# Where layer 1's second chunk keeps its results, and two places in the order of work: a two-layer convolution kernel

## The chip, the cores and the metric

The kernel runs on one core of one Trainium2 chip. The metric is the device time of one execution in microseconds (us); a profiled execution gives, besides its time, the span from its first to its last instruction and the mean clock that was granted to TensorE.

## The reference, cut to what matters

The input x has shape (4, 64, 256, 256). Layer 0 normalises it by groups of channels, runs a gated mixture of small experts behind a 3x3 convolution, and adds the result to x. Layer 1 normalises again and runs two 3x3 convolutions, each followed by a batch normalisation over all four images:

```python
    # --- layer 0 (conv_preact) ---
    x = x + _L0_conv_ref(_gn(x), ...)
    # --- layer 1 (conv_preact) ---
    x = x + _L1_conv_ref(_gn(x), ...)
    ...
    h = _conv3x3(x, _quantize_weight(w1), b1)
    h = jax.nn.relu(_batchnorm(h, gamma1, beta1))
    h = _conv3x3(h, _quantize_weight(w2), b2)
    h = _batchnorm(h, gamma2, beta2)
    return jax.nn.relu(h + identity)
```

In layer 0, a convolution gives h, a 1x1 convolution splits it in two, one half goes through a horizontal and a vertical filter of three taps and a GELU (this is xs), the other half through the experts' low ranks; the experts' sum and xs are projected and added to x. Because a batch normalisation needs the statistics of all images, all of layer 1's first convolution has to be done before its second can begin.

## The kernel before, in words

**Stages.** The four images ("batches" b) are each cut into 16 chunks k of 16 rows; two rows of 64 channels fill the 128 partitions. The time falls into four stages: layer 0's front (to about 1290 us), layer 1's first convolution, called conv1 (to about 1987 us), its second, conv2 (to about 2550 us), and a last stage that reads y and h2 back, normalises and writes the output. The second half of layer 0 (the projection and the sum y = x + ..., called out here) lags behind: its last ten slots of batch 2 (n = 22 to 31) and all 32 slots of batch 3 run in the middle of conv1.

**The order of the work** is written by hand. A plan maps a pair (step, order) to calls (`at`, L120), and when it is complete the calls are made in the order of these keys. Each engine keeps that order in its own queue: PE, DVE (VectorE), ACT (ScalarE), POOL (GpSimd), and SP, which issues most DMAs. So a step number says what comes before what on one engine, not a time; semaphores do the rest. Step `CONV1` = 128, called t below for batch 0, is where conv1 begins; a chunk of conv1 takes four steps. The front's last work is spread over the first steps of conv1 by a table, `TAIL`: for the last chunk but one, the taps' t on ACT (`front_taps_i`, L692) is at (t, 13.3), the rest of the taps on DVE (`front_taps_h`, L699 to L717) at (t, 13.4), and xs on ACT (`front_xs`, L723) at (t, 13.5).

**One chunk of conv1.** `conv1_load` (L905, SP) fetches yn, rows of y, from memory. `conv1_differences` (L343, POOL) makes differences d of rows. `conv1_upper_odd` (L923, L359, ACT) and `conv1_upper` (L346, ACT) round the rows and the differences to the format that PE multiplies fast; `conv1_lower_odd` (L362, DVE) and `conv1_lower` (L353, DVE) keep what the rounding lost. PE then makes `conv1_odd` (ps_hm, 12 matmuls) and twice `conv1_even` (ps_h, 12 matmuls each, g = 0 and 1), all on L296. `conv1_shared` (L312, ACT) turns ps_hm into m; `conv1_out` (L318, DVE) makes h from ps_h and m for g = 0 and 1; `conv1_square` (L382, ACT) adds up squares and then has ACT's queue store h to memory (L985, h_d<-h in the profile).

**Places in SBUF.** A tile with a tag and `bufs=1` has one place; a new tile with the tag waits until all readers and stores of the last one are done. h of a chunk goes into tag "h1" of the conv1 pool (one place), or, for odd k outside the first chunks, into tag "x" of the first pool (one place; in the front it held loads of the out work, `xs_load` with place "x", L837). m goes into tag "k" from chunk (0,2) on, which is also the place of layer 0's rank product, stored by `low_store` (L770, SP, low_d<-k).

**The out work.** `out_load` (L828, SP) reads x's rows into a y tile (tag "o", two places); `xs_load` (L837) and `low_load` (L847) fetch xs and the ranks; a slot n projects on PE (ps_o, L506), adds to y on DVE (L873) and takes statistics (L878). After every second slot `out_store` (L886, SP) writes y to memory (y_d<-y). The function `plan_out_late` places this work in conv1: a slot at its step, with order 13.6, the loads nine and six steps ahead, the store one step behind. An issue on SP whose wait isn't over holds every later issue on SP.

**What the change touches:** `conv1_out` (L961 to L963), the line of `plan_out_late` that places `out_store` (L1195 and L1196), and three lines of `plan_conv1` (L1232, L1233, L1235).

Of the kernel before, what the change touches and what calls it, by code (L numbers as in the profile page):

```python
# [41 lines left out]
def conv_preact_kernel(ctx: ExitStack, tc: tile.TileContext, io, col128, colset, col64):  # L42
# [25 lines left out]
    def flat(t):  # L68
        return t.rearrange("p a b -> p (a b)")
# [23 lines left out]
    def chunk_x(name):  # L93
        return first_pool.tile([P, CPAIR, PW], F32, tag="x", name=name, bufs=1)
# [25 lines left out]
    def at(step, order, call, *args):  # L120
        plan[step, order].append((call, args))
# [194 lines left out]
    def leave(h, ps, m, w, total):  # L316

        nc.vector.scalar_tensor_tensor(  # L318
            h.rearrange("p (e k) w -> p e (k w)", e=2),
            ps.rearrange("p e k w -> p e (k w)"),  # L320
            w_scale[w],
            m.unsqueeze(1).to_broadcast([P, 2, GF]),
            ALU.mult,
            ALU.add,
            **({} if total is None else {"accum_out": total}),
        )
# [45 lines left out]
    def totals_less(name, rows):  # L372

        first = stat.tile([P, 6], F32, tag="first", name=f"first_{name}")
        nc.vector.bn_stats(first, rows)
        mv = stat.tile([P, 2], F32, tag="first_mv", name=f"first_mv_{name}")
        nc.vector.bn_aggr(mv, first)
        nc.vector.tensor_scalar(less[name], mv[:, 0:1], -1.0, None, ALU.mult)
# [514 lines left out]
    def out_end(b):  # L893
        gn2[b] = const.tile([P, 3], F32, name=f"gn2_{b}")
        yield from group_norm(st_y.pop(b), c128("avg4"), gn2[b][:, 0:2], f"y{b}", nc.gpsimd if b < B - 2 else nc.vector)
        (nc.gpsimd if b < B - 2 else nc.vector).tensor_scalar(gn2[b][:, 2:3], gn2[b][:, 0:1], gn2[b][:, 1:2], -1.0, ALU.mult, ALU.mult)
# [63 lines left out]

    def conv1_out(b, k, g):  # L961
        if g == 0:
            if k % 2 and (b > 0 or k > 2):  # L963
                h_out[b, k] = flat(chunk_x(f"h1_{b}_{k}"))[:, 0 : CPAIR * W].rearrange("p (a b) -> p a b", b=W)
            else:
                h_out[b, k] = conv1_pool[0].tile([P, CPAIR, W], F32, tag="h1", name=f"h1_{b}_{k}", bufs=1)
        h = h_out[b, k]
        at_h = h[:, 4 * g : 4 * g + 4, :]
        first = k == g == 0
        total = sums[b][:, 2 * k + g : 2 * k + g + 1]  # L970
        leave(at_h, open_h.pop((b, k, g)), m_in[b, k][:, g], "w1", None if first else total)
        if first:
            nc.vector.tensor_reduce(total, h[:, 1:4, :], AX.XY, ALU.add)
            nc.vector.tensor_reduce(sums[b][0:C, NOCT : NOCT + 1], h[0:C, 0, :], AX.X, ALU.add)
            if b == 0:
                totals_less("h1", h[:, 1:3, :])
        if g:
            del m_in[b, k]
# [59 lines left out]
    def at_each(places, chain):  # L1038

        for place in places:  # L1040
            at(*place, next, chain, None)
# [145 lines left out]
    def plan_out_late(b, ns, steps, order, end):  # L1187

        for n, step in zip(ns, steps):
            if n % 2 == 0:  # L1190
                at(step - 9, 0.2, low_load, b, n // 2)
                at(step - 9, 0.3, xs_load, b, n // 2, "h")
                at(step - 6, 0.4, out_load, b, n // 2)
            at(step, order, out_slot, b, n)
            if n % 2:  # L1195
                at(step + 1, 13.3, out_store, b, n // 2)  # L1196
        at_each(end, out_end(b))

    def conv1_first():
# [12 lines left out]
    def plan_conv1(b):  # L1212
        t = CONV1 + b * (NG + 1)
        if b == 0:
            at(t - 4, -1, conv1_first)
            at(t, 12, conv1_open)
        for k in range(NCH):
            T = t + 4 * k
            places = [T + p for p in (-13, -7, -6, -5, -4, -4, -4, -3)]
            if b == 0 and k < 3:  # L1220
                places = [t + p for p in ((-6, -3, -3, -2, -2, -2, -1, -1), (-4, -1, -1, 0, 0, 0, 0, 1), (-2, 1, 2, 3, 4, 4, 4, 5))[k]]
            load, diff, odd, up0, up1, low_odd, low0, low1 = places

            first = b == k == 0

            def late(step, order):
                return (step, 5.5 + (order - 13) if step < t else order)

            at(load, 0, conv1_load, b, k)
            at(*late(diff, 13.08), conv1_differences, b, k)  # L1230
            at(*late(odd, 13.36 if b == 0 and k == 3 else 13.1), conv1_upper_odd, b, k)
            at(*late(up0, 13.12), conv1_upper, b, k, 0)  # L1232
            at(*late(up1, 13.14), conv1_upper, b, k, 1)  # L1233
            at(*late(low_odd, 13.2), conv1_lower_odd, b, k)
            at(*((t, 1.3) if first else late(low0, 13.22)), conv1_lower, b, k, 0)  # L1235
            at(*((t, 1.32) if first else late(low1, 13.24)), conv1_lower, b, k, 1)
            at(T, 1.9 if first else 13, conv1_odd, b, k)
            at(T + 4 / 3, 13, conv1_even, b, k, 0)
            at(T + 4 / 3, 13.15, conv1_shared, b, k)
            at(T + 8 / 3, 13, conv1_even, b, k, 1)  # L1240
            at(T + 8 / 3, 13.05, conv1_out, b, k, 0)
            at(T + 4, 13.05 if k < NCH - 1 else 12.9, conv1_out, b, k, 1)
            at(T + 4 + 4 / 3, 13.16, conv1_square, b, k)
        at(t + NG, 12.95, conv1_end, b)
        at(t + NG + 1, 13.06, conv1_end_out, b)
        at(t + NG + 3, 13.3, conv1_close, b)

    plan_front()
    for b in range(B):
        if b < B - 1:  # L1250
            plan_stats(b + 1)
            plan_out(b, NOCT if b < B - 2 else 22)
            if b == B - 2:
                plan_out_late(b, range(22, NOCT), [CONV1 + 16 + 4 * n for n in range(10)], 13.6, [(CONV1 + n, 12.6) for n in (56, 58, 58, 60, 60, 60, 62)])
        else:
            t, e = CONV1 + 56, CONV1 + b * (NG + 1) - 10
            steps = [t + (e - 6 - t) * n // (NOCT - 1) for n in range(NOCT)]
            plan_out_late(b, range(NOCT), steps, 13.6, [(e - i, 15) for i in (5, 3, 3, 1, 1, 1, -1)])
        plan_conv1(b)
# [116 lines left out]
    with tc.manual_schedule(  # L1376
# [8 lines left out]
        n = len(chunks)  # L1385
# [186 lines left out]
```

## Time and profile before

| | |
|---|---|
| median of 3 runs | 2990.66 us (2983.44 to 2991.94) |
| the profiled execution | 2990.48 us |
| its span | 2988.7 us, mean granted TensorE clock 0.915 |
| PE, matmuls | 2351.9 us busy (79% of the span) |
| DVE | 2440.1 us (82%) |
| ACT | 2024.8 us (68%) |
| POOL | 1682.5 us (56%) |
| DMA | 915.33 MB, mean 306 GB/s |

Busy shares are means over stages with different limits, so they are read stage by stage. In an instruction's row of a timeline the first two numbers are its start from the beginning of the span and its length in us; then follow engine, line, operation, the tiles it writes and reads, and, in brackets, how long the engine was idle before it and what ended that. A row of the chain of waits has start, length and what the time went to; "DMA a<-b" is a transfer that somebody waited for, from its issue to the end of the wait. A row of the waits names the waiter, what it waited for, the total in us, how many times, and the longest.

### The profile page before, as it was taken

To read this page: it belongs to the slowest core of one execution; us is meant where nothing else is said; L and a number is where in the kernel's file an instruction comes from. 1 tells how busy PE (TensorE), PEld (TensorE's weight loads), DVE (VectorE), ACT (ScalarE), POOL (GpSimd) and SP (SyncE) were. 2 spreads that over 40 slices of the span, in tenths; PEclk is the share of its full clock that TensorE was granted. 3 is DMA by queue.
4 is the path that set the end of the run, shared out by engine and by line. 5 is a ranking of instruction groups with operands and counts; after the bars stand their busy time and mean duration, and the time that the engine had idled before them with its cause. 6 is when DMAs were issued, how large, how long until landed. Compare 5 with 4: busy or idle time off the path is not lost.

```text
span 2988.7 us, 52829 instructions
## 1 busy us (share of the span) xinstructions
PE 2351.9 (79%) x21576; PEld 1500.3 (50%) x21576; DVE 2440.1 (82%) x2754; ACT 2024.8 (68%) x2210; POOL 1682.5 (56%) x1283
## 2 busy tenths in 40 slices
PE   1888899999999999989999999989999999100000
PEld 1444445444444555546666667867888888000000
DVE  5678678878878888868988889979999898876665
ACT  6777888778776665567666667968888888432222
POOL 5888888778778888734544546735555565000000
PEclk9999999999999999999999999989999999555555
DMA  8565579999999899849999997747777763899999
GB/s 348 206 237 209 196 270 370 357 350 353 345 336 321 295 320 323 293 181 323 361 345 358 340 337 275 283 164 269 262 266 263 264 234 140 354 420 425 425 424 407
DMA packets 135570, 915.33 MB, mean 306 GB/s; under 512 B 14944, under 2 KB 15712, under 8 KB 40608
## 3 DMA queue, kind: packets, MB, share of 16 engines
q1 hardware_dynamic: 107680, 777.74, 70.1%
q10 hardware_dynamic: 27648, 134.23, 11.3%
q8 instruction: 169, 2.77, 0.4%
q14 instruction: 73, 0.60, 0.1%
HBM read 573.74 MB, written 338.17 MB: 305 GB/s over the span
## 4 chain that ended last, share of the span: by engine, by line
PE 50%; DMA 27%; DVE 10%; POOL 6%; ACT 3%; issue 3%; SPq 0%; ACTq 0%; DVEq 0%; POOLq 0%
PE ps_h L296 19%; PE ps_c L506 8%; PE ps_a L506 6%; PE ps_h2m L296 6%; DMA y<-in_xp 6%; DMA y_d<-y 5%; PE ps_o L506 5%; DMA y_end<-y_d 5%; DMA out<-h 4%; DMA h<-h_d 4%; PE ps_hm L296 3%; POOL x L554 2%; DMA xs_in<-xs_d 2%; DVE y L873 1%; DVE t L707 1%
## 5 line engine op out<-in xcount | busy, mean ns | idle before, releaser
L296 PE MATMUL ps_h<-diff,w_q 128*128 128x512 f32 x3072 | 756.8, 401 | 17.6 <-DVE h L318 17.2
L296 PEld LDWEIGHTS ps_h<-diff,w_q 128*128 128x128 f32 x3072 | 578.9, 190 | 196.1 <-issue 28.8
L506 PE MATMUL ps_c<-v,us 64*64 64x256 f32 x9216 | 538.4, 382 | 28.6 <-DVE ps_c L637 23.8
L343 POOL TENSOR_TENSOR d<-yn 128x1024 f32<-128x1024 f32 x128 | 347.8, 2738 | 305.6 <-DMA yn<-y_d 189.8
L506 PEld LDWEIGHTS ps_c<-v,us 64*64 64x64 f32 x9216 | 359.3, 135 | 180.5 <-DVE ps_c L637 24.2
L506 PE MATMUL ps_a<-h,av 64*64 64x512 f32 x4080 | 388.0, 494 | 55.2 <-DVE t L710 40.1
L343 POOL TENSOR_TENSOR d<-h 128x1024 f32<-128x1024 f32 x127 | 311.9, 2478 | 194.8 <-DVE diff L351 133.3
L318 DVE SCALAR_TENSOR_TENSOR h<-ps_h,scale_w,m 128x1024 f32<-128x1024 f32 x256 | 322.8, 1279 | 73.3 <-PE ps_h L296 53.4
L554 POOL TENSOR_TENSOR x<-x 128x512 f32<-128x512 f32 x256 | 330.0, 1289 | 12.5
L1453 ACT ACTIVATE v<-y_end,shift,gn 128x2048 f32<-128x2048 f32 x64 | 133.8, 2093 | 280.2 <-DMA y_end<-y_d 245.1
L506 PEld LDWEIGHTS ps_a<-h,av 64*64 64x64 f32 x4080 | 153.8, 133 | 331.6 <-issue 203.5
L382 ACT ACTIVATE junk<-h,less_h 128x2048 bf16<-128x2048 f32 (+3 forms) x133 | 255.9, 1924 | 11.1 <-DVE h L318 10.9
L1454 DVE SCALAR_TENSOR_TENSOR h<-h,ss,v 128x2048 f32<-128x2048 f32 x64 | 149.8, 2349 | 121.4 <-ACT v L1453 96.8
L692 ACT ACTIVATE t<-ps_a,tap_bias,m 128x1016 f32<-128x1016 f32 x128 | 153.4, 1199 | 128.7 <-PE ps_a L506 99.7
L873 DVE SCALAR_TENSOR_TENSOR y<-ps_o,ob,y 128x1024 f32<-128x1024 f32 x128 | 163.9, 1280 | 74.8 <-PE ps_o L506 26.8
L723 ACT ACTIVATE xs<-t 128x1024 f32<-128x1024 f32 x128 | 134.8, 1053 | 102.3 <-DVE t L710 88.4
L296 PE MATMUL ps_h2m<-odd,w_q 128*128 128x512 f32 x768 | 193.2, 401 | 8.2 <-DVE odd L362 4.4
L296 PE MATMUL ps_hm<-odd,w_q 128*128 128x512 f32 x768 | 191.4, 398 | 2.8 <-DVE t L710 1.3
L353 DVE SCALAR_TENSOR_TENSOR diff<-d,gn,diff 128x1024 fp32r<-128x1024 f32 x128 | 192.3, 1531 | 0.5 <-ACT diff L346 0.5
L346 ACT ACTIVATE diff<-d 128x1024 fp32r<-128x1024 f32 x128 | 135.1, 1056 | 83.3 <-POOL d L343 82.1
L546 POOL TENSOR_TENSOR x<-x,x 128x512 f32<-128x512 f32 x128 | 160.9, 1280 | 22.2 <-ACT x L540 22.2
L296 PEld LDWEIGHTS ps_h2m<-odd,w_q 128*128 128x128 f32 x768 | 146.3, 191 | 44.5 <-DVE odd L362 5.2
(250 smaller groups left out, 4271.5 us busy)
## 6 DMA issues: line engine op xcount, KB each, us to landing
x<-in_xc SPq DMA_DIRECT2D x64, 1280.0 KB
h<-h_d SPq DMA_DIRECT2D x64, 1152.0 KB
yn<-y_d SPq DMA_DIRECT2D x60, 1152.0 KB
xs_in<-in_xp SPq DMA_DIRECT2D x64, 1024.0 KB
xs_d<-xs ACTq DMA_DIRECT2D x128, 512.0 KB
xs_in<-xs_d SPq DMA_DIRECT2D x64, 1024.0 KB
y<-in_xp SPq DMA_DIRECT2D x64, 1024.0 KB
y_d<-y SPq DMA_DIRECT2D x64, 1024.0 KB
```

The lines of the kernel that those rows point to most:

```text
L296: nc.tensor.matmul(ps, wq[w][:, kind, kx, :], t[:, rows, kx : kx + W], start=(j == 0), stop=(j == len(terms) - 1))
L318: nc.vector.scalar_tensor_tensor(h.rearrange("p (e k) w -> p e (k w)", e=2), ps.rearrange("p e k w -> p e (k w)"), w_scale[w], m.unsqueeze ...
L343: engine.tensor_tensor(raw.rearrange("p (g r) w -> p g r w", g=2), *pair, ALU.subtract)
L346: nc.scalar.activation(inner(tiles[0], 4 * n, 4 * n + 4), raw, AF.Copy, scale=scale)
L353: nc.vector.scalar_tensor_tensor(lower, raw, scale, upper.bitcast(F32), ALU.mult, ALU.subtract)
L382: nc.scalar.activation(junk[rows, 0:n], flat(h), AF.Square, bias=less[name][rows], accum_out=total)
L506: last[:] = [nc.tensor.matmul(ps[o, at_out[0] : at_out[1], :], w[i], rhs[i], **flags)]
L546: nc.gpsimd.tensor_tensor(x4[:, j - 1], x_rows(u, j + 2), x4[:, j - 1], ALU.subtract)
L554: nc.gpsimd.tensor_tensor(x[:, r : r + 2], x[:, r + 2 : r + 4], x[:, r : r + 2], ALU.subtract)
L692: nc.scalar.activation(t[:, :, inside], ps[:, :, inside], AF.Identity, bias=tap_bias, scale=sh[:, 1:2])
L873: nc.vector.scalar_tensor_tensor(y, ps.rearrange("p x s w -> p x (s w)"), out_bias[b], y, ALU.add, ALU.add)
L1454: nc.vector.scalar_tensor_tensor(h, h, ss2[:, 0:1], v, ALU.mult, ALU.add)
```

## The change

It has three parts.

1. The results h of chunk 1 of batch 0 are put into the place of tag "x", as those of chunk 3 and of all later odd chunks are already; before, they went into the place of tag "h1", like chunks 0 and 2.
2. For the same chunk (b = 0, k = 1), at step t, the two calls of `conv1_upper` move from orders 13.12 and 13.14 to 13.36 and 13.37, and the first `conv1_lower` from 13.22 to 13.45. The taps' t has 13.3, the taps' work on DVE 13.4 and xs 13.5 in that step.
3. In `plan_out_late` the store of y goes to two steps behind the slot, where it was one.

```diff
     def conv1_out(b, k, g):
         if g == 0:
-            if k % 2 and (b > 0 or k > 2):
+            if k % 2:
                 h_out[b, k] = flat(chunk_x(f"h1_{b}_{k}"))[:, 0 : CPAIR * W].rearrange("p (a b) -> p a b", b=W)
             else:
                 h_out[b, k] = conv1_pool[0].tile([P, CPAIR, W], F32, tag="h1", name=f"h1_{b}_{k}", bufs=1)
...
             at(step, order, out_slot, b, n)
             if n % 2:
-                at(step + 1, 13.3, out_store, b, n // 2)
+                at(step + 2, 13.3, out_store, b, n // 2)
...
+            behind = b == 0 and k == 1
-            at(*late(up0, 13.12), conv1_upper, b, k, 0)
-            at(*late(up1, 13.14), conv1_upper, b, k, 1)
+            at(*late(up0, 13.36 if behind else 13.12), conv1_upper, b, k, 0)
+            at(*late(up1, 13.37 if behind else 13.14), conv1_upper, b, k, 1)
             at(*late(low_odd, 13.2), conv1_lower_odd, b, k)
-            at(*((t, 1.3) if first else late(low0, 13.22)), conv1_lower, b, k, 0)
+            at(*((t, 1.3) if first else late(low0, 13.45 if behind else 13.22)), conv1_lower, b, k, 0)
```

By the plan's steps, part 3 lets nine loads pass ahead of a store of y in SP's queue: the load of yn of the even chunks of batch 2 (eight, at steps 117 to 173, ahead of the store that was placed one step earlier) and one load of xs of batch 3 (step 54, ahead of the last store of batch 2). The other stores keep their neighbours.

## The prediction

> **What bounds the kernel now.** I read the page's 40 slices first, then the chain that ended last, then around the weakest slice the timelines of PE, DVE, ACT and SP, and at last the waits. Except in the hand-over from layer 0 to layer 1 (about 1297 to 1360 us) and the memory-bound last stage, PE is busy nearly all the time. The stretches, with the columns us, PE, PEld, DVE, ACT, POOL busy (instructions), granted clock, DMA share, GB/s:
>
> ```profile
> 1290.00:1365.00 75.00, 59.33 (x324) 36.94 (x324) 50.66 (x58) 45.69 (x49) 30.80 (x17) 0.89 0.62 220
> 1365.00:1640.00 275.00, 266.31 (x1316) 180.88 (x1309) 247.39 (x290) 191.84 (x183) 130.78 (x49) 1.00 0.93 348
> 1640.00:1830.00 190.00, 176.84 (x855) 120.39 (x853) 168.31 (x182) 125.61 (x122) 91.64 (x36) 0.98 0.90 331
> ```
>
> In the hand-over PE lacks 15.7 of 75 us and the clock is down. The chain of waits there (start, us, what):
>
> ```profile
> 1302.01 0.23 DVE t L699
> ...
> 1305.01 4.55 PE ps_a L506 x24
> ...
> 1336.93 2.95 DMA low_d<-k
> ...
> 1340.05 10.54 DMA h_d<-h
> ...
> 1352.07 8.68 PE ps_h L296 x24
> ```
>
> Layer 0's last tap sums (t, L699 to L710) feed PE, then the last ranks' store frees the tile that layer 1's m needs, then a store of h1 takes 10.54 us with everybody waiting. That store is chunk (0,1)'s: its tile tag "h1" has one buffer, and chunk (0,2)'s L318 at 1350.72 writes it next. PE's own view (last bracket: idle before, and what ended it):
>
> ```profile
> 1305.01 4.55 PE L506 MATMUL ps_a<-h,av 64*64 64x512 f32 x24 [3.40 <-DVE t L710]
> 1320.25 2.38 PE L506 MATMUL ps_a<-h,av 64*64 64x512 f32 x24 [1.00 <-DVE t L710]
> 1352.07 8.68 PE L296 MATMUL ps_h<-diff,w_q 128*128 128x512 f32 x24 [7.76 <-DVE h L318]
> 1365.59 5.90 PE L296 MATMUL ps_h<-diff,w_q 128*128 128x512 f32 x24
> ```
>
> The same 24 matmuls take 2.38 us after 1.00 us of idle and 4.55 after 3.40; the other 24 take 5.90 and, after 7.76 of idle, 8.68. And the start of the tail, ACT and DVE together:
>
> ```profile
> 1297.98 2.20 ACT L346 ACTIVATE diff<-d,gn 128x1024 fp32r<-128x1024 f32 x2 [0.87 <-POOL diff L90]
> 1299.23 2.86 DVE L353 SCALAR_TENSOR_TENSOR diff<-d,gn,diff 128x1024 fp32r<-128x1024 f32 x1 [0.54 <-ACT diff L346]
> 1300.08 1.18 ACT L692 ACTIVATE t<-ps_a,tap_bias,m 128x1016 f32<-128x1016 f32 x1
> 1302.01 0.22 DVE L699 SCALAR_TENSOR_TENSOR t<-ps_a,m,edge_bias 128x8 f32<-128x8 f32 x1
> ```
>
> Layer 1's uppers (L346) hold ACT before the taps' t (L692), and its lower (L353) holds DVE until 1302.01 although t was there at 1301.26.
>
> **What the skill says.** The Trainium skill's "TensorE: Matmul & The Clock Gate", Part 1 (the HAM clock gate), says that TensorE falls to half its clock after an idle window of some 3.4 us and recovers after about as long of work. The trace agrees with the direction: slow after 3.40 and 7.76 us idle, not after 1.00; the edge is not sharp (12 ps_h took 4.59 us after 2.46 idle at 1665.47, but 3.06 after 2.38 at 1608.52). "DMA: Bandwidth & Descriptors", section "Issuing engines are not separate DMA queues", says that DMAs of SP and ACT share the same 16 DMA engines. The trace agrees: the 1024 KB of h_d took 10.54 us at 1340.05, when SP had just been released and issued six loads within 3 us.
>
> **Edit 2, the uppers behind the taps' t.** On ACT the two L346 (2.20 us) now follow L692, on DVE one L353 follows L699 to L710; nothing is added. PE ends the taps' last 8 matmuls at 1298.60 (1297.94 + 0.66), so t runs 1298.63 to 1299.83. DVE has then finished the lower odd (1297.51 + 1.19 = 1298.70), so L699 starts at 1299.86 and not 1302.01: **2.15 us** earlier. The uppers fill ACT's wait for DVE's L710 (the idle 3.68 us before xs at 1304.94; they need 2.20 of the 2.87 that DVE takes), and their reader, chunk (0,1)'s matmuls, comes only at 1322.56: cost nothing. If that cover were gone, xs would come up to 2.2 us late, and xs is next read by ps_q at 1333.53.
> PE's 3.40 us of idle before 1305.01 becomes 3.40 − 2.15 = 1.25, near the 1.00 that left the clock alone. So I take the warm times: 4.55 − 2.38 = 2.17 on ps_a and 3.53 − 3.08 = 0.45 on the ps_h x12 behind it (rows at 1309.48 and 1298.53), together **2.62 us**. Bounds: 0 if the clock still drops, 2.62 if not. From there to the ranks' store at 1336.93 every step on the chain waits for the one before (ACT k, t, DVE t, PE, with 0.41 us on ACT as the least spare), so all of it moves 2.15 + 2.62 = 4.8 us earlier, the low_d store and SP's queue behind it too.
>
> **Edit 1, (0,1)'s h in the place of x.** No instruction is added. Chunk (0,1) now waits for the last reader of the x place (layer 0's projections of slot 61, over 30 us before), chunk (0,2) for the store of (0,0), issued 1325.29 and with its last packets near 1330: both long past. So (0,2)'s L318 waits for m alone (m ends at 1341.18, less 4.8 is 1336.4). PE then goes from ps_hm (1341.23 + 3.07) straight into ps_h: its idle **7.76 us** is gone, and with it the cold start, 8.68 − 5.89 = **2.79 us**.
> The wait doesn't vanish, it moves: chunk (0,3) now writes x behind (0,1). The store is issued at 1340.05 − 4.8 = 1335.3 and, at the same 10.54 us, lands at 1345.8. DVE wants to write (0,3) after h(0,2) twice, a lower odd held by ACT until about 1340.6, two lowers and the gate's spread: about 1346.8. One microsecond of spare; the landing may be 0 to 4 us later in the same burst, and PE reads the bank that this frees only at about 1350.7, so I take 0 and keep 3 as the bad end.
> What is late next: ps_g and odd (0,4) on PE at 1345.8 against 1360.59, that is 15 us earlier; the y and yn that the first out slots need were issued at 1337 to 1343 and are 4.8 us earlier, used some 12 us or more after landing. The next store on SP (1377.57, waiting for the y sum) and all loops behind it follow the compute.
> Sum of edits 1 and 2: 2.15 + 2.62 + 7.76 + 2.79 = **15.3 us**.
>
> **Edit 3, out_store a step later.** Same DMAs; only what SP issues between step + 1 and step + 2 changes place. Worked out from the plan: eight loads yn of batch 2 (even chunks, at steps 117, 125 ... 173) and one xs_in (step 54) now go ahead of a y_d store; POOL, ACT and PE queue nothing there. SP stands at those stores for the y sum, and POOL stands for yn:
>
> ```profile
> SPq L886 <- DVE y L873: 82.1, 8, 15.7
> SPq L828 <- DMA y_d<-y: 44.5, 7, 12.0
> ```
>
> ```profile
> POOL d L343 <- DMA yn<-y_d: 101.9, 16, 15.2
> ```
>
> (both 1640 to 1870 us; total, times, longest). The eight loads go out some 5 to 15 us sooner (for instance behind the y load at 1714.62 instead of behind the store at 1729.41), and the xs_in behind the store (25.04 us to land at 1708.80) gets a shorter queue. PE's gaps in 1640:1830 are 190 − 176.84 = 13.2 us: no more can come back. Against it: a yn ahead of the store is 1152 KB, at 331 GB/s 3.6 us, and the y loop (store, landing, y load into the same tile) is on the chain at one such store (1636.20, 15.37 us). DMA share is already 0.90, so order helps only part of the gaps. I take **−4 us**, bounds −10 and +7 (one 3.6 for yn, 3.2 for xs_in).
>
> Sum: 15.3 + 4 = 19.3. The profiled execution took 2990.48 (span 2988.7, 1.8 us around it), 0.2 under the median of 2990.66 of the three runs, which reach from 2983.44 to 2991.94. 2990.5 − 19.3 = 2971.2, said as **2971.5**. About 0.3% (9 us) is what a measurement of this kernel can tell from no change.
>
> **Rivals.**
> - Half the gain: the clock still drops (2.62 lost), (0,3) waits for (0,1)'s store (3 lost) and edit 3 brings nothing (4 lost): 2971.2 + 9.6 = about 2981. For it: one microsecond of spare at the store, the blurred edge of the clock. Against: PE's need of that bank comes 4 us later.
> - The memory takes it back: with a DMA share of 0.93 from 1365 to 1640, a start 15 us earlier only meets y and yn that are not there yet, the stalls at 1431 and 1444 grow, and some 5 us remain: 2985.5. For it: the share. Against: the loops start with a store that waits for the compute, so the traffic starts earlier too, and DMA is at 0.46 from 1365 to 1375.
> - Slower: yn ahead of the store lengthens the y loop each time. Place: SP's queue at the eight stores of steps 116 to 172. Price 3.6 us each, 28.8 in all, and it decides when yn can't go before the y sum is ready (its ring place is freed by a lower odd three chunks back), so that yn and the store are issued together. Then 2990.5 − 15.3 + 28.8 = 3004. Against: the places are free at 1697 and 1715 by the timelines, and only one of these stores is on the chain.
> - That the edits don't act: (0,1) is the chunk whose store is waited for, so I give this no chance of its own.
>
> **Numbers.** The forecast 0.68, half the gain 0.15, memory 0.12, slower 0.05. Faster by over 0.3% (below 2981.7): all of the forecast and most of the second, 0.81; within: 0.14; slower 0.05. The range takes the forecast with its bounds (edit 3 to −10: 2965, with 4 us for the scatter of single runs 2961) up to 2984, which holds the second rival and the edge of the third.
>
> **What would show it.** L692 ahead of L346 and t at about 1299.9; 24 ps_a in 2.4 us; no DMA wait before (0,2)'s L318, and at (0,3)'s one of at most 3 us; PE's idle of 7.76 us gone; ps_g 15 us earlier; fewer POOL waits for yn after 1640. Wrong if chunk starts near 1640 are less than 10 us earlier, or if PE's gaps between there and 1830 exceed 13 us.

## The result, and the profile after

| | median | range | runs |
|---|---|---|---|
| kernel before | 2990.66 us | 2980.63 to 2994.01 | 7 |
| changed kernel | 2971.94 us | 2966.09 to 2983.91 | 7 |

The changed kernel is faster: ratio 0.9959, 95% interval 0.9939 to 0.9979, so 12.3 us with 6.3 to 18.2. The two medians lie 18.7 us apart, which is more than the ratio says; seven runs each with a spread of some 14 us leave that much open.

The profiled execution of the changed kernel took 2983.91 us (span 2982.1), the slowest of its seven. Its front, up to the first matmul of conv1, took 3.0 us longer than in the profile of before, and its last, memory-bound stage 7.7 us longer. Neither stage is touched by the change, and over all profiles of this study the two run from 1281.4 to 1296.6 us and from 434.4 to 443.2 us, whatever the edit. So the stages are compared below from mark to mark, not by their absolute times.

The three stretches of the hand-over and of conv1 in the changed kernel (columns us, busy time of PE, PEld, DVE, ACT and POOL with instructions, granted clock, DMA share, GB/s):

```profile
1290.00:1365.00 75.00, 69.13 (x418) 43.26 (x411) 57.93 (x71) 53.75 (x57) 36.95 (x20) 1.00 0.69 244
1365.00:1640.00 275.00, 261.28 (x1274) 177.48 (x1276) 249.58 (x279) 186.73 (x179) 127.36 (x48) 0.99 0.94 353
1640.00:1830.00 190.00, 183.80 (x897) 127.33 (x890) 174.62 (x193) 135.31 (x132) 105.67 (x40) 1.00 0.89 346
```

In the first, PE lacks 5.9 us where it lacked 15.7, and the clock is full. In the third it lacks 6.2 where it lacked 13.2. But in the second it lacks 13.7 where it lacked 8.7: something was given back there. PE's own view shows the hand-over (last bracket: idle before, and what ended it):

```profile
1305.89 2.38 PE L506 MATMUL ps_a<-h,av 64*64 64x512 f32 x24 [1.30 <-DVE t L710]
1342.44 5.78 PE L296 MATMUL ps_h<-diff,w_q 128*128 128x512 f32 x24
1348.05 0.28 PE L785 MATMUL ps_g<-m,spread 128*128 128x9 f32 x2
1353.13 5.89 PE L296 MATMUL ps_h<-diff,w_q 128*128 128x512 f32 x24
```

The 24 ps_a are warm again after 1.30 us of idle, and the 24 ps_h that had cost 8.68 us behind 7.76 of idle take 5.78 behind none. ACT and DVE show the two edits that did it, first ACT, then DVE:

```profile
1301.65 1.20 ACT L692 ACTIVATE t<-ps_a,tap_bias,m 128x1016 f32<-128x1016 f32 x1 [1.63 <-PE ps_a L506]
1302.74 2.19 ACT L346 ACTIVATE diff<-d,gn 128x1024 fp32r<-128x1024 f32 x2
```

```profile
1339.45 1.28 DVE L318 SCALAR_TENSOR_TENSOR h<-ps_h,scale_w,m 128x1024 f32<-128x1024 f32 x1 [2.10 <-ACT m L312]
1349.83 1.28 DVE L318 SCALAR_TENSOR_TENSOR h<-ps_h,scale_w,m 128x1024 f32<-128x1024 f32 x1 [1.44 <-DMA h_d<-h]
```

The taps' t now goes ahead of the uppers. Chunk (0,2)'s L318 (the first of the two DVE rows) waits for m alone. In the kernel before it waited for (0,1)'s store:

```profile
1350.72 1.28 DVE L318 SCALAR_TENSOR_TENSOR h<-ps_h,scale_w,m 128x1024 f32<-128x1024 f32 x1 [11.61 <-DMA h_d<-h]
```

The wait for a store has moved to chunk (0,3), the second row, where it is 1.44 us and PE is not held by it. And the chain of waits of the changed kernel (start, us, what) names what is late next:

```profile
1302.88 0.24 DVE t L699
...
1305.89 2.38 PE ps_a L506 x24
...
1335.18 2.94 DMA low_d<-k
...
1347.25 27.73 DMA yn<-y_d
...
1375.11 5.79 POOL d L343 x2
```

The store of h is gone from it, and in its place stands a load of yn, chunk (0,8)'s, that took 27.73 us from its issue. Nothing like it was on the chain of before at this place.

The same in a table of stages. Each stage runs from one mark to the next; the marks are the first ps_hm, the issue of the ranks' last store (L770), the gate's ps_g (L785), and the h of chunks (0,12), (1,12) and (2,13). In brackets stands the difference to the profile of before, in us; the last columns are the sum of the five differences, and what the times say (ratio times the median of before on the same chip, with its interval).

| kernel | to L770 | to ps_g | to (0,12) | to (1,12) | to (2,13) | sum | by the times |
|---|---|---|---|---|---|---|---|
| before | 45.2 | 23.7 | 97.3 | 179.5 | 193.8 | | |
| changed kernel | 40.5 (−4.7) | 12.9 (−10.8) | 103.6 (+6.3) | 181.5 (+2.0) | 183.9 (−9.9) | −17.1 | −12 (−18 to −6) |
| after_again, the same once more | 40.4 (−4.8) | 12.8 (−10.8) | 104.3 (+7.0) | 181.7 (+2.2) | 183.1 (−10.7) | −17.1 | −14 (−21 to −8) |
| e1_x_place | 45.1 (−0.1) | 14.2 (−9.4) | 102.1 (+4.8) | 180.5 (+1.0) | 191.8 (−2.0) | −5.7 | −4 (−8 to +1) |
| e2_taps_first | 40.5 (−4.7) | 22.0 (−1.6) | 97.0 (−0.3) | 180.9 (+1.3) | 189.9 (−3.9) | −9.2 | −4 (−8 to +1) |
| e3_store_late | 44.3 (−0.9) | 22.0 (−1.6) | 96.9 (−0.4) | 182.0 (+2.5) | 184.2 (−9.6) | −10.0 | −6 (−10 to −2) |
| e4_one_and_two | 40.6 (−4.6) | 14.2 (−9.5) | 101.8 (+4.5) | 179.9 (+0.4) | 192.6 (−1.2) | −10.4 | −7 (−11 to −3) |
| f1_early_loads | 40.6 (−4.6) | 15.5 (−8.2) | 97.8 (+0.5) | 181.5 (+2.0) | 183.0 (−10.8) | −21.1 | −25 (−29 to −20) |
| f1_again, the same once more | 40.5 (−4.7) | 16.5 (−7.2) | 97.9 (+0.6) | 181.3 (+1.8) | 184.9 (−8.9) | −18.4 | −17 (−23 to −10) |
| f3_two_early | 40.5 (−4.7) | 14.2 (−9.4) | 97.9 (+0.6) | 181.2 (+1.7) | 185.3 (−8.5) | −20.3 | −18 (−25 to −11) |
| f2_early_loads_before | 54.2 (+9.0) | 25.5 (+1.8) | 97.1 (−0.2) | 181.3 (+1.8) | 192.3 (−1.5) | +10.9 | +10 (+7 to +14) |
| g_store_tail | 40.5 (−4.7) | 12.9 (−10.8) | 103.5 (+6.2) | 185.7 (+6.2) | 183.7 (−10.1) | −13.2 | −21 (−26 to −16) |
| h_store_six | 40.5 (−4.7) | 12.8 (−10.8) | 106.0 (+8.7) | 204.5 (+25.0) | 204.8 (+11.0) | +29.2 | +29 (+24 to +34) |

The sums and the times go the same way in every row, and for the changed kernel and its parts the sum is some 2 to 6 us larger. All sums are taken against one profile of before, and that one is not typical in every stage. It drew longer cold starts than e2 and e3 at the same idle (last section), which accounts for the −1.6 that even these show at ps_g. Its 193.8 us to (2,13) are some 2 more than the mean of the four other profiles without part 3 (e1, e2, e4 and f2: 189.9 to 192.6), and its 179.5 us to (1,12) some 1 less. For f1 and g the times give 4 and 8 us more than the stages; both were measured on one chip, on which the changed kernel was not.

### The profile page after: what moved, and what is told of

It is laid out like the page before. It is cut to its first block, busy times and chain, and to the rows that moved or that the text cites. A ratio compares the mean times of both kernels' runs of the same rounds, so it can differ in the third digit from the quotient of the medians.

```text
span 2982.1 us, 52815 instructions
## 1 busy us (share of the span) xinstructions
PE 2346.5 (79%) x21576; PEld 1496.4 (50%) x21576; DVE 2441.6 (82%) x2754; ACT 2023.1 (68%) x2210; POOL 1688.5 (57%) x1283
## 4 chain that ended last, share of the span: by engine, by line
PE 46%; DMA 29%; DVE 11%; POOL 6%; ACT 4%; issue 4%; SPq 0%; ACTq 0%; DVEq 0%; POOLq 0%
PE ps_h L296 17%; PE ps_c L506 8%; DMA y<-in_xp 7%; PE ps_a L506 6%; PE ps_h2m L296 6%; DMA y_d<-y 6%; DMA y_end<-y_d 5%; DMA h<-h_d 4%; PE ps_o L506 4%; DMA yn<-y_d 3%; DMA out<-h 3%; PE ps_hm L296 2%; POOL x L554 2%; DVE y L873 1%; DVE t L707 1%
## 5 line engine op out<-in xcount | busy, mean ns | idle before, releaser
L296 PE MATMUL ps_h<-diff,w_q 128*128 128x512 f32 x3072 | 753.6, 399 | 12.3 <-DVE h L318 12.1
L506 PEld LDWEIGHTS ps_c<-v,us 64*64 64x64 f32 x9216 | 358.5, 135 | 180.9 <-DVE ps_c L637 23.8
L318 DVE SCALAR_TENSOR_TENSOR h<-ps_h,scale_w,m 128x1024 f32<-128x1024 f32 x256 | 322.8, 1279 | 64.6 <-PE ps_h L296 54.8
L382 ACT ACTIVATE junk<-h,less_h 128x2048 bf16<-128x2048 f32 (+3 forms) x133 | 256.0, 1924 | 11.1 <-DVE h L318 10.9
```

The lines of the kernel that those rows point to most:

```text
L296: nc.tensor.matmul(ps, wq[w][:, kind, kx, :], t[:, rows, kx : kx + W], start=(j == 0), stop=(j == len(terms) - 1))
L318: nc.vector.scalar_tensor_tensor(h.rearrange("p (e k) w -> p e (k w)", e=2), ps.rearrange("p e k w -> p e (k w)"), w_scale[w], m.unsqueeze ...
L382: nc.scalar.activation(junk[rows, 0:n], flat(h), AF.Square, bias=less[name][rows], accum_out=total)
L506: last[:] = [nc.tensor.matmul(ps[o, at_out[0] : at_out[1], :], w[i], rhs[i], **flags)]
```

## The experiments

**The parts one at a time.** Three kernels have one part of the change each, and one has the first two together. Part 1 alone:

```diff
-            if k % 2 and (b > 0 or k > 2):
+            if k % 2:
```

> Edit 1 alone (chunk (0,1)'s h in the place of x). Theory of the prediction: the 24 ps_a at 1305 stay slow (4.55 us, 3.4 us idle), but PE's idle of 7.8 us before ps_h of chunk (0,3) and the cold start behind it (2.8 us) go, so ps_g comes 10.5 us sooner, counted from the first ps_hm; of that some 3 us are given back by 1640, the time is 2983 (7 to 8 us less). Rival (the wait only moves to chunk (0,3), which writes x next): ps_g at most 5 us sooner and a wait of 5 us or more on the store before (0,3)'s h; the time within 3 us of before.

Measured: 2981.76 us (22 runs), ratio 0.9988 (0.9972 to 1.0003). The hand-over to ps_g is 9.4 us shorter, and 4.8 of it come back before (0,12). The cold start on the taps' matmuls stays, since part 2 is not there; PE in this kernel:

```profile
1301.71 4.55 PE L506 MATMUL ps_a<-h,av 64*64 64x512 f32 x24 [3.41 <-DVE t L710]
```

So the x place does what was predicted in its own stage, and about half of what it wins is lost in the next one. The whole time alone would not tell this kernel from the one before, since its interval reaches past 1.

Part 2 alone (the three lines of `plan_conv1`, with orders 13.36, 13.37 and 13.45 for chunk (0,1)):

> Edit 2 alone (uppers behind the taps' t). Theory: t 2.15 us sooner, the 24 ps_a warm (2.38 us instead of 4.55), so the ranks' store is issued 4.8 us sooner, counted from the first ps_hm; the wait of 10.5 us for (0,1)'s store stays with its cold start of 2.8 us, ps_g is 4.8 us sooner, the time 2987 (3 to 4 us less). Rival (the clock drops whatever the 2 us): ps_a stays at 4.5 us and everything moves by 2.2 us alone.

Measured: 2982.63 us, ratio 0.9988 (0.9974 to 1.0002). The ranks' store goes out 4.7 us earlier, and DVE then waits as before for the store of (0,1); DVE in this kernel:

```profile
1335.47 1.28 DVE L318 SCALAR_TENSOR_TENSOR h<-ps_h,scale_w,m 128x1024 f32<-128x1024 f32 x1 [11.42 <-DMA h_d<-h]
```

The gain of part 2 doesn't depend on part 1, and nothing of it is taken back in the stage behind. This interval, too, reaches past 1: the gain is read from the stage, not from the time.

Part 3 alone:

```diff
-                at(step + 1, 13.3, out_store, b, n // 2)
+                at(step + 2, 13.3, out_store, b, n // 2)
```

> Edit 3 alone (out_store a step later). Theory: nothing up to chunk (0,13); between chunk (1,12) and chunk (2,13) some 4 us less (the forecast) to 10 us less (as the changed kernel's profile has it), the time 2982 to 2987. Rival 1: the order on SP changes nothing, the 10 us in the changed kernel's profile come from the phase in which edits 1 and 2 leave the transfers; time within 2 us of before. Rival 2: a yn ahead of each store lengthens the y loop, time 5 us or more above before.

Measured: 2980.58 us, ratio 0.9979 (0.9965 to 0.9993). The stage to (2,13), where eight of the nine loads pass a store, is 9.6 us shorter than in the profile of before. Taken against all five profiles without part 3 (189.9 to 193.8 us), the seven profiles with it (183.0 to 185.3; h left out) are some 8 us shorter.

Parts 1 and 2 without part 3:

> Edits 1 and 2 without edit 3. Theory: ps_g 15.3 us sooner, counted from the first ps_hm; some 5 us given back by 1640, and nothing gained between (1,12) and (2,13); time 2980 (10 us less), so 4 to 10 us above the changed kernel. Rival (edit 3 is nothing): the same time as the changed kernel, and the stretch (1,12) to (2,13) as short as in its profile.

Measured: 2980.73 us, ratio 0.9976 (0.9962 to 0.9991). The two parts add up to 14.1 us at ps_g, 4.5 come back before (0,12), and the stage to (2,13) stays as it was (−1.2). So the gain there in the changed kernel is part 3's. The waits of SP from 1640 to 1870 us (total, times, longest) say it too, first without part 3 (e4), then with it alone (e3), then in the changed kernel:

```profile
SPq L886 <- DVE y L873: 80.3, 8, 15.5
```

```profile
SPq L828 <- DMA y_d<-y: 72.2, 7, 12.9
SPq L886 <- DVE y L873: 42.1, 8, 14.6
```

```profile
SPq L828 <- DMA y_d<-y: 70.4, 7, 14.4
SPq L886 <- DVE y L873: 44.7, 8, 15.4
```

SP stands half as long for the y sum (82.1 us before), because it comes to that wait a step later, behind the loads of yn. The wait for the store's landing at the next y load (L828) grew from 44.5 us by about 26 to 28: the time is partly moved. That it costs less there, because no yn that is late stands behind it, is argued and not shown. POOL's waits for yn are a weak sign here: they fell from 101.9 us to 65.6, but without part 3 also, in e4 to 71.2 and in e2 to 60.4, and the changed kernel has one more of 13.6 us that the view puts down to another releaser.

**What was given back, and why.** The first four kernels put the loss behind part 1 and ahead of (0,12). The chain names a load of yn. It is the last of eight loads that SP issues within 12.1 us once the ranks' store is out of its queue (1335.18): y, two yn, two of ranks, xs, y, yn. Before that, the DMA engines are lightly used: in the kernel before, their share from 1300 to 1340 us is 0.35. If the loads are the cause, three of them that need not wait for that store (the y of the first late slots and yn of chunks (0,6) and (0,7)) can be placed ahead of it. First in the changed kernel:

```diff
-            at(load, 0, conv1_load, b, k)
+            at(t + 9 if b == 0 and k in (6, 7) else load, 0, conv1_load, b, k)
...
-                at(step - 6, 0.4, out_load, b, n // 2)
+                at(step - (8 if n == 22 and b == B - 2 else 6), 0.4, out_load, b, n // 2)
```

> The changed kernel, with three loads (y of the first late slots, yn of chunks (0,6) and (0,7)) ahead of the ranks' store in SP's queue instead of behind it. Theory: the 6 us that the changed kernel gives back between ps_g and chunk (0,12) are transfers that still start behind the ranks' store, at most 5 us sooner, and land too late for a compute that is 15 us sooner; moved ahead into the idle stretch of the DMA engines they are out of the way, so that stretch goes from 103.6 back to about 98 us and the time is 5 us under the changed kernel (some 17 under before). Rival (it is given back by the steady loops of store and load, or by the gate's small operations on DVE): that stretch stays at 102 to 104 us and so does the time.

Measured: 2966.07 us (2961.60 to 2967.68, 5 runs), ratio 0.9917 (0.9902 to 0.9933). The stage to (0,12) is 97.8 us against 103.6, as long as before the change. That stage, from ps_g to the h of (0,12), in the kernel before, in the changed kernel and in this one:

```profile
1360.59:1457.89 97.30, 97.30 (x482) 67.14 (x481) 89.84 (x106) 70.63 (x66) 44.82 (x18) 1.00 0.89 336
1348.05:1451.66 103.61, 99.75 (x499) 67.71 (x497) 95.34 (x110) 73.84 (x71) 49.44 (x19) 1.00 0.95 344
1338.18:1435.96 97.78, 97.34 (x480) 67.15 (x481) 92.13 (x110) 73.70 (x70) 46.04 (x18) 1.00 0.87 330
```

PE lacks nothing in the first, 3.9 us in the second and 0.4 in the third. (The other 2.4 us of the 6.3 are 17 matmuls more: at that mark, which is DVE's, PE was further ahead of DVE.) So the place of these loads behind the ranks' store is what cost the time. Whether they hurt by starting late or by crowding the stage is not separated: by the last two columns the DMA engines were busier in the changed kernel (0.95 against 0.89 and 0.87) and moved some 35.6 MB in its stage, against 32.7 and 32.3. The load that was late points to the crowd. Chunk (0,8)'s yn is issued 52.5 us after the first ps_hm in the changed kernel and 52.3 us after it in f1, so it starts no earlier; but it takes 15.0 us to land in place of 27.7, and POOL, which makes the differences of (0,8) from it, waits for DVE and not for it. POOL in f1:

```profile
1355.94 2.47 POOL L343 TENSOR_TENSOR d<-yn 128x1024 f32<-128x1024 f32 x1 [3.85 <-DVE diff L353]
```

The edit costs something as well: ps_g comes 15.5 us behind the ranks' store and not 12.9. One part is that this store now shares the engines with a load issued just ahead of it; ACT in this kernel:

```profile
1327.64 1.20 ACT L312 ACTIVATE m<-ps_hm,m,scale_w 128x1024 f32<-128x1024 f32 x1 [7.75 <-DMA low_d<-k]
```

In the changed kernel this wait was 5.85. The other part, 1.3 us, is in e1, e4 and f3 as well (14.2): there, as here, ps_g waits for the gate's spread on DVE, which takes 2.45 us or more where the changed kernel takes 0.29 (last section). Counted from the first ps_hm to (0,12), with the later ps_g in it, f1 is ahead of the changed kernel by 3.1 us.

Then the same three loads in the kernel before:

> The same three loads ahead of the ranks' store, in the kernel before. Theory: (0,1)'s store, which chunk (0,2) waits for there, meets 3.3 MB less in the DMA engines and lands 4 to 7 us sooner, so ps_g is 4 to 7 us sooner and the time 3 to 5 us under before. Rival (the store's 10.5 us are not from the crowd): ps_g as before, time as before.

Measured: 2999.50 us (22 runs), ratio 1.0035 (1.0023 to 1.0047), slower. In the kernel before, each of the first stores of h, issued by ACT, has a chunk's L318 behind it, and loads of SP beside it make it longer. That the two share the engines is what the Trainium skill's "DMA: Bandwidth & Descriptors", section "Issuing engines are not separate DMA queues", states, and here it has a price: (0,0)'s store takes 10.66 us to land, where in the kernel before it took 3.85. DVE in this kernel:

```profile
1330.70 1.28 DVE L318 SCALAR_TENSOR_TENSOR h<-ps_h,scale_w,m 128x1024 f32<-128x1024 f32 x1 [5.15 <-DMA h_d<-h]
1356.71 1.28 DVE L318 SCALAR_TENSOR_TENSOR h<-ps_h,scale_w,m 128x1024 f32<-128x1024 f32 x1 [13.99 <-DMA h_d<-h]
```

Chunk (0,1) now waits for (0,0)'s store, with the ranks' k (L764) queued behind it on DVE, so that the ranks' store goes out 9.0 us later. Of these, 5.15 us are the wait; the other 3.9 are two operations between it and k, the lower odd and a lower, which took 1.22 and 1.28 us before and take 2.92 and 3.47 with POOL's d now beside them. And chunk (0,2) waits 13.99 us where it waited 11.61. The early loads gain some 3 us in the changed kernel and cost 10 in the kernel before. The three loads were therefore not what made (0,1)'s store slow: without them it lands in 12.9 us in place of 10.5, beside the four loads that are still issued with it (two of ranks, xs, y).

Last, only two of the three loads early (`k == 6` for `k in (6, 7)`), so that none lies just ahead of the ranks' store; with it the changed kernel and f1 once more, on one chip:

> As before, but only y and yn of chunk (0,6) go ahead of the ranks' store; yn of (0,7), which was issued 2.3 us ahead of it and stood in its way, goes behind again. Theory: m's wait for low_d is back at 5.9 us, ps_g 2 us sooner than with three loads, the rest as with three; time 1 to 2 us under f1. Rival: yn of (0,7) then delays the loads behind it and 2 to 4 us are given back before (0,12).

> The three early loads in the changed kernel, once more, beside it. Theory: 4 to 6 us under the changed kernel (6 given back no longer, 2 lost at the ranks' store, behind which m waited 7.75 us instead of 5.85). Rival: the lead over the changed kernel came from another chip; within 2 us of it.

> The changed kernel itself, beside the two versions below on the same chip. Theory: by the stages it is 13 to 15 us faster than before (12 to 15 in the hand-over, less 6 and 2 given back, and 10 in the stretch (1,12) to (2,13)); a time that is 6 us faster at most would mean that the stages in the profiles are not typical.

Measured: f3 2966.93 us (2960.71 to 2983.34, 8 runs), ratio 0.9939 (0.9915 to 0.9963); f1 2970.25, ratio 0.9944 (0.9922 to 0.9966); the changed kernel 2975.01, ratio 0.9952 (0.9931 to 0.9973). In f3 ps_g is back at 14.2 us and the stage to (0,12) stays at 97.9; that stage in f3:

```profile
1342.42:1440.30 97.88, 97.88 (x482) 67.40 (x482) 91.28 (x109) 72.89 (x69) 46.98 (x18) 1.00 0.89 335
```

PE lacks nothing there. The stage is settled in three profiles of kernels with early loads (97.8, 97.9, 97.9) against two without (103.6, 104.3). The whole times don't settle it: in this second comparison the intervals of all three overlap. What the early loads are worth on top of the change is 3 to 5 us when the stages up to (0,12) are added up, since ps_g comes later (f1 3.1, f1_again 2.7, f3 4.9, each against the changed kernel of its comparison), and by the times 2 (f1_again) and 4 (f3) on the same chip. The lead of 13 that the last column of the table gives f1 is one across two chips. In the second profile of the changed kernel, POOL's wait carries the load's name:

```profile
1370.57 5.83 POOL L343 TENSOR_TENSOR d<-yn 128x1024 f32<-128x1024 f32 x2 [13.87 <-DMA yn<-y_d]
```

In the first profile the same idle (12.24 us) was put down to DVE's odd, L362, though the yn had landed 0.13 us before it ended: a wait for several semaphores, of which the view names one.

**How far a store can go back.** Part 3 leaves the five late stores of batch 2 with their old neighbours, except for one load of xs that passes the last of them. In one kernel these too go behind the next load of yn:

```diff
-                at(step + 2, 13.3, out_store, b, n // 2)
+                at(*((step + 3, 0.1) if b == B - 2 else (step + 2, 13.3)), out_store, b, n // 2)
```

> The changed kernel, with the five late stores of batch 2 also placed behind the next load of yn (at step 3, order 0.1), as part 3 of the change has it for eight stores further on. Theory (a yn must not stand behind a store that waits for the y sum): ps_g to (0,12) 3 to 6 us shorter than the changed kernel's 103.6, time 3 to 6 us less. Rival (the y loop bounds that stretch): as long or longer.

Measured: 2968.72 us, ratio 0.9930 (0.9914 to 0.9946). By the stages the five moves bring nothing: 103.5 us to (0,12) against 103.6, and 185.7 to (1,12), 4.2 more than in the changed kernel. The time is within the changed kernel's own range, but against before on its own chip it is 21 us shorter (16 to 26), more than its stages say. As the changed kernel was not measured on that chip, it stays open whether the moves bring anything.

In the other, all stores go back until just ahead of the load that needs their place:

```diff
-                at(step + 2, 13.3, out_store, b, n // 2)
+                at(step + (5 if b == B - 2 else 6), 0.1, out_store, b, n // 2)
```

> The changed kernel, with each late store moved on until just ahead of the y load that needs its place (past the xs load and one more yn). Theory: the store is then on the way of the y loop, the y load waits its whole landing of about 15 us each time, and the stretches ps_g to (2,13) grow by 15 us or more; time 10 us or more above the changed kernel. Rival (stores are never urgent; what counts is that loads go first): time as the changed kernel or some us less.

Measured: 3021.27 us (3013.73 to 3024.28), ratio 1.0097 (1.0079 to 1.0115), slower than before by 29 us. The three stages of conv1 are 8.7, 25.0 and 11.0 us longer than before. SP's waits from 1640 to 1870 us in this kernel:

```profile
SPq L828 <- DMA y_d<-y: 156.3, 8, 26.0
```

The wait for a store's landing is 70.4 us in the changed kernel. Now nearly all of SP's standing is here, with every load of yn behind it. The y loop of the rival is real, but in these runs it sets in only when the store is put just ahead of its own y load with nothing between, not when one load of yn passes it.

## Why the prediction was right or wrong

**Edit 2** was right in mechanism and size: the ranks' store 4.8 us earlier was forecast, 4.7 was measured, in e2, in the changed kernel and again in after_again, with the 24 ps_a at 2.38 us. The Trainium skill's "TensorE: Matmul & The Clock Gate", Part 1, holds here in its direction: 1.30 us of idle left the clock alone, 3.41 in e1 did not. Some luck was in it: in f2 the 24 ps_h at 1332.05 took 7.41 us in place of 5.89 behind only 1.90 us of idle.

**Edit 1** was right where it acts: 7.76 + 2.79 = 10.6 was forecast and 10.8 measured, 9.4 in e1. The 1.3 us more in the changed kernel go with the quick spread, so they are not the edit's own. The wait moved to (0,3) with 1.44 us in the changed kernel, between the 0 taken and the 3 kept as the bad end, and in e1 and e4 with none. PE did not feel it, as was argued.

**The step that failed** is "What is late next". It took the loads issued at 1337 to 1343 as "4.8 us earlier, used some 12 us or more after landing", and left out the next one on SP, chunk (0,8)'s yn, issued at 1354.42. By the landings in the trace of before, that yn came at 1374.43, only 1.5 us ahead of its use at 1375.90, and chunk (0,6)'s 7.7 us ahead of its own. In the changed kernel, counted from the first ps_hm, (0,8)'s yn is issued 10.1 us earlier, but it meets the loads behind the ranks' store, which start only some 4.7 us earlier. It takes 27.7 us in place of 20.0 and lands 2.4 us earlier, while POOL is ready for it 16 us earlier. What was spare before became a wait: POOL idle 12.24 us, and 6.3 to 7.0 us of the stage given back. That is the rival "the memory takes it back" in kind, a start that "only meets y and yn that are not there yet", with the DMA share of the stage up from 0.89 to 0.95, though not in size: it ends on some 7 us of the 15, and f1 and f3 show that the place of a few loads decides. The reason against that rival, that traffic starts with the compute, was true of the stores and not of the loads behind L770.

One of the prediction's own signs of being wrong came true with it: chunk (1,12), near 1640, is 7.2 us earlier counted from the first ps_hm (6.4 in after_again), less than the 10 that it asked for. The other, gaps of over 13 us in PE from there to 1830, did not: they are 6.2.

**Edit 3** was right in mechanism, and its size is the mis-sized term: 4 was taken. Measured against the one profile of before it was 10 (9.6 in e3, 9.9 and 10.7 in the changed kernel), against all five profiles without part 3 some 8; e3's time gives 6, with 2 to 10. The bound was taken from PE's gaps (13.2 us, 6.2 after it), and the discount on it for a DMA share of 0.90 was too large: at 0.89 half of the gaps closed. The price of 3.6 us for a yn ahead of the store, the slower rival's, did not show; h shows what would have brought it. A further +2.0 us to (1,12), which e3, f1 and f3 have as well, is not explained; as e2 and f2, without part 3, have +1.3 and +1.8, much of it belongs to the one profile of before.

**The sum** of 19.3 us was 17.1 by the stages, twice, and 12 to 14 by the times; it lies above the interval of the ratio, which ends at 18.2. The errors of the failed step (6 to 7 us too much) and of edit 3 (4 to 6 too little) nearly cancelled, and the medians lie further apart than the ratio says, so the forecast of 2971.5 beside a median of 2971.94 is largely luck; in the second comparison the changed kernel took 2975.01. Of the 3 to 5 us between stages and times, some 2.5 are what the one profile of before has more than its like; the rest stays open.

The kernel that the experiments point to is f3: the change with one y and one yn ahead of the ranks' store. Its median is the lower one of the two on the same chip, but its lead over the changed kernel is not resolved by the times.

## What to carry to other kernels

When an edit brings a consumer forward by 15 us, ask of each transfer that it reads what releases its issue, whether that comes forward by as much, and what will be in the DMA engines ahead of it; slack in the old profile is slack only against the old consumer. Loads in a queue behind a store that waits for compute start with that store, so while the DMA engines have little to do ahead of it, that is the place to put them, unless a store on the critical path lies there too: the same loads gained 3 to 5 us in the changed kernel and cost 10 in the kernel before. And order in an issuing queue can be worth gaps of the compute engine at a DMA share of 0.9, as long as a store isn't put just ahead of the load that needs its place.

## What the hardware showed that was not expected

The length of a cold stretch varies at the same idle. The 24 ps_a behind 3.40 or 3.41 us of idle took 4.55 us in the profile of before, in e1 and in f2, and 3.61 in e3; the 24 ps_h took 8.68 us after 7.76 of idle, but 7.19 after 7.60 in e3 and 7.27 after 7.54 in e2. The granted clock in the traces goes with it. In each of the 13 profiles it is either full or half, and it changes only at whole multiples of 3.41 us from its other changes. The ps_a had 6.83 us of half clock in before, e1 and f2, and 3.41 in e3; the ps_h had 10.24 in before and 6.83 in e2 and e3. So what a stall costs depends also on where it falls between these steps, and a cold start read from one profile is uncertain by 1 to 1.5 us.

A small operation of DVE, the gate's spread (L781, 128x128), took 2.45 to 2.49 us in nine profiles and 0.29 in four. In all nine, one of POOL's d starts 0.05 us ahead of it and ends some 0.1 us ahead of its end (in f3 POOL from 1339.86 to 1342.29, the spread from 1339.91 to 1342.37); in the four no d runs beside it, as POOL still waits for yn. The two slow operations of DVE in f2, above, had a d beside them too. No run was made to separate the two engines, so the link is only observed.

The two loads of ranks and the y, xs and yn beside them moved slowly: from 1353 to 1362 us the changed kernel's DMA engines were busy to over 90% at 188 to 266 GB/s, against 403 to 434 in the ten microseconds ahead. It may be one reason for the 27.73 us of the yn; it wasn't tried alone.
